# Three of six units of a depthwise convolution on VectorE, LN2's normalisation and a bias on ScalarE, and a product in two 64-row tiles

## The chip, the cores and the metric

One core of one Trainium2 chip runs the whole program. The metric is the device time in microseconds of one execution. Five engines work side by side, each in its own fixed order of instructions: TensorE (PE, with its weight loads PEld), VectorE (DVE), ScalarE (ACT), GpSimd (POOL) and SyncE (SP, which here only issues DMAs).

## The reference

The input is 32 images of 56 x 56 pixels with 96 channels. Every image goes through two layers:

```python
# layer 0: an inverted residual with mixed experts (E = 4, M = 384)
rw = sigmoid(mean(x) @ Wr + br)                  # four weights per image
h = relu(bn1(x @ (rw . Wpw) + rw @ bpw))         # 96 -> 384 channels
h = relu(bn2(sum_e rw[e] * (dw3x3(h, Wdw[e]) + bdw[e])))   # depthwise, 3 x 3, 'SAME'
x = bn3(h @ (rw . Wpwl) + rw @ bpwl) + x         # 384 -> 96
# layer 1: a mixer by Fourier transform over all 3136 tokens, then a feed-forward
t = tokens(x)
u = relu(bn(ln(t) @ w1))                         # 96 -> 192
X = fft(u, axis=tokens, norm='ortho')
xr = relu(X.real * rd - X.imag * id + rb)        # diagonals of r and i
xi = relu(X.imag * rd + X.real * id + ib)
t = t + bn2(ifft(xr + 1j * xi).real @ w2)        # 192 -> 96
z = float8_e5m2(ln(t))                           # LN2 is this ln
z = relu(fp16(fp16(z @ W1) + fp8(b1)))           # 96 -> 384, h in fp16
t = t + fp16(fp16(fp8(z) @ W2) + fp8(b2))        # 384 -> 96
```

## The kernel before

**Staging.** Channels lie on partitions, an image is cut into two halves by columns (h = 0, 1), each with its own padded tile `x0`, `x1`, and each half into two stretches (`st` = 0 to 3). `record(b)` writes down the steps of one image; all 32 are written down before anything is issued.

**The conditional convolution.** The 384 channels are three groups of 128 (c = 0, 1, 2); a half image and a group together are a *unit*, six per image. There are two forms of a unit. `by_tensor` expands 96 to 128 channels in 32-column tiles (`x,wk` 32x435, 16 matmuls), spreads the four pixels of every 2 x 2 square over partitions by DMA (`hp<-h`), convolves as 64 matmuls of 32x32 tiles (`hp,wg`) with weights that GpSimd builds, evicts with bias and relu on ScalarE (`hp<-ps,small`) and sends the result back by DMA (`h<-hp`). `by_vector` expands with full 128-column matmuls (464 and 406 columns), makes the middle tap with its bias on ScalarE (`h<-h,small`), adds eight taps for each of two stretches on VectorE (`h<-h,small,h`, 16 instructions of 784 elements) and ends with a relu on ScalarE (`h<-h`). `BY_VECTOR` says which units are of the second form: group 2 of each half (`DC = 2`). The projection of a half (`project`) runs over the three groups into four banks of PSUM, from 32-row tiles (`h,wk`) or, for a by_vector unit, whole (`h,wkc`); `landed` adds it to `x`.

**The Fourier mixer.** `moments` turns tokens with the identity, takes their statistics on VectorE, and their root on GpSimd (`root`, a power of -1/2). `hidden`, `scaled` and `along_h` make the first transform's direction, which goes through DRAM (`gd`). Then seven groups of frequencies (`GROUPS`: six of four and one of five) each run `along_q` (the second direction: 128 channels in `za`, the last 64 in `zb`, two frequencies sharing one tile of 128 partitions, 64 rows each), nine steps of the filter on ScalarE and VectorE, `second` (the product with `w2`, in one bank for a group of four), `back_q` and a DMA to `yd`.

**The tail.** For each stretch: `back_h`, the residual, `moments` again (LN2), `normal` (seven instructions per stretch, `nt<-ps,ln`), `turn_back`, the feed-forward: `up`, a copy of h to fp16 on ScalarE (`h16`), bias and relu on VectorE (`h<-h,fb`), a cast to fp8 on GpSimd, `down`, bias and residual.

**What sets the order.** Each step is an entry of a `Plan`, with an engine, a cost in microseconds, a due time and the buffers that it takes. `Plan.order()` plays all steps through once before the kernel is built: an engine that comes free takes, of the first 60 ready steps by due time, the first whose buffers are free. The order found is then issued to the engines as it is (`Pinned`), so that the profile puts nearly all instructions on one line, that of the helper. The due times come from `WANT` (a period per image and offsets of the parts), a table of corrections `NUDGE`, one per step in turn, and

```python
if eng in ("DVE", "ACT") and any(isinstance(k[0], Buf) and isinstance(k[0].ring, Banks) for k in reads):
    due -= HURRY
```

which moves the steps that read PSUM ahead. `LAG` is the planner's time from an end to a dependent start on another engine. PSUM is a ring of eight banks (`Banks`), from which a step takes one, two (a neighbouring pair) or four; `r_h` holds three expanded units.

Of the kernel before, what the change touches and what calls it, by code (L numbers as in the profile page):

```python
# [11 lines left out]
F32 = mybir.dt.float32  # L12
F16 = mybir.dt.float16
E5M2 = mybir.dt.float8e5
AF = mybir.ActivationFunctionType
# [3 lines left out]
NE = 4  # L19
C = 96  # L20
# [21 lines left out]
DC = 2  # L42
NT = NC3 - 1
NG = 4 * NT
# [110 lines left out]

LANES = 8
# [4 lines left out]
def packets(n, size):  # L161
# [7 lines left out]
WANT = dict(period=120.2, expand=0.0, vector=1.4, forward=10.7, forward_step=27.0, freq=172.2,  # L169
            freq_step=7.0, tail=259.2, tail_step=26.5, x=17.0, mix=33.5, project=33.0)  # L170

HURRY = 115.8
# [6 lines left out]
    18.3, -16.9, 17.3, 0, -35.5, 15.1, -2.2, -43.4, 13.8, 5.4, 60.8, 7.8, -0.2, -11.5, 4, 4.7, -13.1, -0.5,  # L179
    18.6, 17.1, 11.1, 10.2, -11, 20.5, -10.1, 14.1, -21.4, 3.4, -7.5, 17.2, 4.5, 21.7, 18.3, 11.9, -19.7, 22.1,  # L180
    11.4, 0, -2.1, 49.4, -19.6, 9.4, -26.2, -6.4, 9.1, 3.3, 5.5, 5, 21.1, 20.3, 33.2, -7, 5.8, -11.9,
    16.3, -7.5, 3.9, -11.5, 12.5, -4.7, 8.9, -4.9, 17.9, 27.4, -6.8, 18.5, -3.3, 11.3, 28.7, 17.7, 19.5, 44.7,
    16.4, 1.2, 9.3, -0.3, 19.5, -5.2, 17.7, -40.7, 8.8, -11.7, -4.1, -9.1, -20.5, -7.9, 1.7, 4.5, -4.4, -8.8,
    3.4, 24.1, 10.9, 14.8, 2, -5.6, 1.7, 0.7, -28.5, -26.6, -32.6, -10.9, 13.4, -39.7, 11.4, 3.2, 6.1, -5.6,
    -2.4, -8.8, 4, 16, -5.7, 18.6, 16.8, 28.3, 33, 30.6, 44.6, 31.5, 16.1, 24.8, 20.3, 36.5, 24.6, 16.1,
    18.6, 42.7, 23.9, 27.6, -3.5, 18.6, -17.7, 2.5, 5.3, 14.5, -0.8, -3.7, 17.7, 9.8, -4.6, 2, 0, 23.1,
    3.5, 21.5, 38.9, 28.4, 44.9, 18.8, 22.4, 26.6, -19, -32.5, -1.9, -10.7, -7.8, 9.5, -10.4, -3.8, -2.9, 8,
    18.9, 13.5, 3.1, 7.3, 8.9, 7, 8.1, 16.4, 11.1, -3.4, -3.1, 20.3, -22.7, -7.6, -24.5, -27.4, -36.4, -34.1,
    -7.3, -20.6, 1.7, 21.7, 20.8, 7.7, 9.3, -5.2, 21.2, 1.1, 2, -16.9, -20.2, -3, 25.2, 3, -24.4, -16.8,
    -12.7, -3.5, 8.7, 1, 23.4, 0.5, 36.6, 13.9, -3.3, 18.2, -6, -15.4, -28, -3.3, -1, 17.1, -0.1, -10.8,  # L190
    -6.3, -25.1, 5.2, -1.4, 8.7, 26.7, -2.7, 31.5, -8.7, -20.5, 17.7, 4.2, -5.4, -11.3, -32.3, 6.6, 36.1, -6.7,
    -16, -33, -18.4, -5.3, 5.5, 6, 28.7, 0, 19.4, 2.9, -31.5, 1.2, -19.7, -10.4, -31.4, -34.5, -8.8, 28.8,
    -34.6, -24.7, -20.9, -38.6, -59.8, -23.4, -15.1, -3, -7.9, -34.5, -56.8, -18.7, 2, -3.6, 10.8, -11.1, 7, 8,
    12.5, -7.2, -61.1, -21.9, 10.6, -3.6, 5.1, -0.2, 3.8, -23.7, -10.7, 25.8, -39.1, -3.1, 3.5, 8.3, -0.9, -28.2,
    -40.3, -3.1, 6.2, 5.8, -18.2, 2.1, -4.7, 20.6, 13.6, -4.8, -49.9, -11.8, 33.8, 6.2, 3.1, -12.4, -19.8, -2.2,
    -15.5, 31.7, -33.1, 12, -1.1, 5.2, -15.6, -56.7, -33.2, -4.2, -6, 0.3, -24.5, -5.5, 1.3, 6.7, -3.6, -23,
    -40.1, 0.5, 32.2, 12.1, -12.4, 0.6, -15.2, 1.8, -11.6, 25.9, -25.3, -0.3, -13.6, 11.9, -9.8, -30.8, -60.1, -29.8,
    9.3, 6.2, -6.3, -5.5, -22.1, 12.9, -5.4, -21.4, -61.3, -2.3, 28.4, 10.6, -0.7, -0.3, 2.2, -3.7, -13.8, 45.6,
    -30.6, -1.8, 4.8, 20.9, -13.9, -4.2, -50.9, -12.3, 5.2, 21, -0.3, 0.1, 0.6, 16.1, -14, -20.6, -90.4, -5.2,
    3.7, 4.1, 4.4, -11.5, -3.2, -9.8, -23.9, 38, -24.6, 0.3, -15.5, 7.6, 5, -33.5, -53.7, 2.4, 3.3, 3.5,  # L200
    7.4, 6.3, 12.4, 55.3, 31.8, -20.5, -60.3, -4.5, 17.2, 12.9, 4.9, 11.6, 7.1, -5.1, 6.7, 49.7, -19.7, -2.1,
    12.4, 19.1, -9.6, -27.1, -37, -5.2, 8.4, 12.9, 1, 2.8, -16.1, 18.1, 26.9, 0.5, -23.1, 12.4, -39.5, -5,
    8.3, 3.6, 2.3, -7.3, -10.6, 32.4, 10.2, 3.2, 23.3, -1.6, 4.1, -6.5, 0, 12.6, 37.9, -9.8, -31.5, 2.8,
    5.4, 3.4, -11.1, 10.2, 4.5, 5, -3.7, 14.2, 0.9, -11.5, -3.6, 7.3, 10.4, -10.2, -6.8, 38.5, -53.4, 21.2,
    3, -4, -2.4, 17.2, -7.6, -23.2, -13.5, -17.6, -5.3, 19.8, -18.8, -48.7, 11.7, 1.6, -11, -29.3, 21.3, -5.8,
    -12.2, -1, 41.3, 3.3, -11.9, 3.1, 14.2, 2.1, 3.7, -0.2, 4.7, -56, 58.2, 18.7, 18.6, 18.1, 20.1, -8.6,
    -31.7, -8.6, 13.1, 0.1, 23.5, -8.6, -37.4, 10.2, 2.8, -13.7, -14.1, -4.3, -14.4, 3.5, 2.7, 28.4, 7.8, 5.6,
    -4, -11.5, 1.5, -5.5, 4.2, 2, -45, 20.5, 28.6, 35.4, 4.9, 21.3, -1.2, -21.7, -3.5, -6.1, 0.7, 40.2,
    -17.3, -21.9, 8.1, 1.8, -10.1, 17.2, -4.1, -5.9, -4.4, 3.6, 20.7, 6.6, 5, 16.3, 25.7, 1.8, -8.5, -1.2,
    -26.7, -59.5, 30.7, -19.7,  # L210
# [4 lines left out]
class Plan:  # L215
# [49 lines left out]
    def order(self):  # L265
# [64 lines left out]
        while events:  # L330
            now = events[0][0]
            while events and events[0][0] <= now:
# [3 lines left out]
                elif kind == "end":  # L336
                    for a in x.after:
                        a.left -= 1
                        lag = LAG["SP"] if x.size else 0.0 if a.eng == x.eng else LAG[x.eng]
                        a.ready = max(a.ready, now + lag + a.slack)  # L340
                        if a.left == 0:
                            push(a.ready, "ready", a)
# [39 lines left out]
def kernel(  # L382
# [58 lines left out]
    stk16 = const([128, NE + 1, NSM + 10], F32, "stk16")  # L441
# [4 lines left out]
    w2b = const([128, 2, C], F32, "w2b")  # L446
# [38 lines left out]
    with tc.tile_pool(name="prep", bufs=1) as pp:  # L485
# [65 lines left out]
        nc.vector.memset(w2b, 0.0)  # L551
        nc.scalar.dma_start(w2a[0:C], w2t[:, 0, :])
        nc.scalar.dma_start(w2a[C:128], w2t[0:32, 1, :])
        for j in range(2):
            nc.scalar.dma_start(w2b[64 * j : 64 * j + 64, j], w2t[32:C, 1, :])
# [60 lines left out]
        for c in range(NT):  # L616
# [3 lines left out]
        nc.vector.tensor_scalar_mul(  # L620
            stk16[:, 0:NE, NSM : NSM + 9], rawp[:, 9 * DC : 9 * DC + 9].rearrange("p k e -> p e k"), s2[:, DC : DC + 1]
        )
        nc.vector.tensor_scalar_mul(stk16[:, 0:NE, NSM + 9], rawp[:, 10 * NC3 + DC], s2[:, DC : DC + 1])
        nc.vector.tensor_copy(stk16[:, NE, NSM + 9 : NSM + 10], sh2[:, DC : DC + 1])
# [55 lines left out]
        for j in range(2):  # L680
            nc.vector.tensor_mul(w2b[:, j], w2b[:, j], scrow)
# [29 lines left out]
    r_small = places(2, [128, NSM + 10], F32, "small")  # L711
# [44 lines left out]

    PERIOD = WANT["period"]
    BY_VECTOR = ((0, DC), (1, DC))

# [4 lines left out]
    def record(b):  # L764
# [68 lines left out]
        def mix_wk2():  # L833
# [8 lines left out]
            "DVE", 2.49, t0 - WANT["mix"], lambda: mixed(wk.ap, wpw_s, wpw_s[:, NE], C + 1), port=True,  # L842
# [23 lines left out]
        def by_vector(h, c, due, acc):  # L866

            hv = Buf(r_h)
            edges = (0, 8, 16, 23, 30)
            for i in range(4):  # L870
                ps, n = Buf(banks), edges[i + 1] - edges[i]

                def expand(i=i, n=n, ps=ps):
# [10 lines left out]
                    "ACT", cols("ACT", n * (S + 2)) + 0.12, due - 4,  # L884
# [6 lines left out]
            def taps(i, tap):  # L891
# [3 lines left out]
                return src, to, small.ap[:, NSM + tap : NSM + tap + 1]  # L895

            def first(i):
                src, to, w = taps(i, 4)
                se.activation(to, src, AF.Identity, scale=w, bias=small.ap[:, NSM + 9 : NSM + 10])
# [25 lines left out]
        def by_tensor(h, c, due, hid):  # L925
# [11 lines left out]
            for g in range(4):  # L937
# [3 lines left out]
                def expand(g=g, ps=ps, chan=chan):  # L941
# [14 lines left out]
                    "ACT", cols("ACT", 435), due - WANT["expand"] + 1,  # L956
# [16 lines left out]
            def conv():  # L973
# [13 lines left out]
                "PE", 3.75, due, conv, reads=[(wg, 0), *((hp, r) for r in range(4))],  # L987
# [23 lines left out]
        for h in range(2):  # L1011
# [3 lines left out]
            for c in range(NC3):  # L1015
                if plain[c]:
                    by_vector(h, c, t0 + h * PERIOD / 2 + WANT["vector"], hid[c])
# [561 lines left out]
```

## Time and profile before

| | |
|---|---|
| median of 3 runs | 4438.66 us (4423.89 to 4443.58) |
| the profiled execution | 4444.37 us, span 4442.5 us |
| busy | TensorE 90%, VectorE 80%, ScalarE 56%, GpSimd 32% of the span |
| mean granted TensorE clock | 0.962 |
| DMA | 734.08 MB, 165 GB/s |
| share of the chain that ended last | TensorE 52%, VectorE 18%, ScalarE 10%, DMA 9% |

A row of a group of instructions reads: engine, operation, the tiles written and read (buffer numbers left out; `ps` is PSUM), the shapes, the count, then the busy time in all and the mean duration in ns, then the idle time of the engine just before them and what ended it. A float32 matmul stands in the trace as two rows. Busy time is the union of overlapping instructions, so that sixteen small matmuls side by side count once. A row of waits reads: who waited, for whom, us in total, times, the longest. A row of the timeline: start and length in us, engine, operation, tiles, shape of the first of the piece, how many instructions.

### The profile page before, as it was taken

The page shows a single profiled execution, that of the slowest core. Times are in us where ns is not written, and L with a number is a line of the kernel's source. Part 1 is how long each engine was busy: PE and PEld are TensorE (multiplying, and loading weights), DVE is VectorE, ACT ScalarE, POOL GpSimd, SP SyncE. Part 2 cuts the span into 40 slices and gives each one's busy share as a digit, 9 for nine tenths or more (in the row PEclk, how much of TensorE's full clock was granted, in tenths as well). Part 3 has the DMA queues.
Part 4 walks back from the last instruction along what each step waited for, and adds up shares of the span by engine and source line. Part 5 has one row for each costly group of instructions (what it writes and reads, how often), then busy time and mean ns, then how long its engine had stood idle before and what let it go on. Part 6 is the DMA issues. An engine that isn't in the chain of part 4 may idle for free.

```text
span 4442.5 us, 114026 instructions
## 1 busy us (share of the span) xinstructions
PE 4003.5 (90%) x44802; PEld 2605.1 (59%) x44802; DVE 3535.3 (80%) x9669; ACT 2507.0 (56%) x4975; POOL 1432.2 (32%) x1364
## 2 busy tenths in 40 slices
PE   2998999999999999999999999899999999999985
PEld 1555665566665566666556666566666566565564
DVE  5777887888878888888888787787887887877864
ACT  2455665565665556666556565455665556565543
POOL 1123333333333333333333323333333333233323
PEclk9999999999999999999999998899999999999996
DMA  5876678767778777777877767667778777677752
GB/s 119 178 163 147 159 179 183 164 165 170 165 175 188 172 173 178 166 169 182 184 166 168 171 160 170 151 165 171 164 175 190 167 169 170 153 171 177 162 142 69
DMA packets 440074, 734.08 MB, mean 165 GB/s; under 512 B 159158, under 2 KB 294774, under 8 KB 439494
## 3 DMA queue, kind: packets, MB, share of 16 engines
q1 hardware_dynamic: 433920, 722.30, 70.4%
q8 instruction: 354, 5.80, 0.6%
q10 hardware_dynamic: 5618, 4.49, 0.4%
q14 instruction: 182, 1.49, 0.1%
HBM read 300.21 MB, written 211.04 MB: 115 GB/s over the span
## 4 chain that ended last, share of the span: by engine, by line
PE 52%; DVE 18%; ACT 10%; DMA 9%; issue 4%; POOL 4%; SPq 1%; POOLq 0%; ACTq 0%; DVEq 0%
PE ps L376 52%; DMA g<-gd 6%; POOL ln L376 4%; DVE za L376 3%; ACT h L376 3%; DVE h L376 3%; DVE ha L376 3%; DVE ln L376 2%; DVE tmpa L376 2%; ACT tmpa L376 2%; DVE zb L376 2%; SPq L376 1%; DMA yt<-yd 1%; ACT za L376 1%; DVE tmpb L376 1%
## 5 line engine op out<-in xcount | busy, mean ns | idle before, releaser
L376 DVE SCALAR_TENSOR_TENSOR h<-h,small,h 128x784 f32<-128x784 f32 x1024 | 1064.2, 1051 | 48.5 <-ACT h L376 29.3
L376 POOL CAST h<-h 128x784 fp8e5<-128x784 f16 x384 | 413.9, 1082 | 989.7 <-DVE h L376 986.5
L376 PE MATMUL ps<-x,wk 97*32 97x435 f32 (+2 forms) x4608 | 680.9, 575 | 14.7 <-ACT h L376 11.1
L376 PE MATMUL ps<-hp,wg 32*32 32x392 f32 x16384 | 518.9, 516 | 36.8 <-issue 25.4
L376 PE MATMUL ps<-dftb_s,g 112*128 112x112 f32 (+1 forms) x3776 | 427.2, 284 | 60.8 <-DMA g<-gd 36.1
L376 ACT ACTIVATE h<-ps 128x435 f32<-128x435 f32 (+2 forms) x768 | 397.7, 541 | 109.9 <-PE ps L376 103.1
L376 PEld LDWEIGHTS ps<-dftb_s,g 112*128 112x128 f32 (+1 forms) x3776 | 356.3, 171 | 167.6 <-issue 100.7
L376 POOL TENSOR_TENSOR ln<-ln,mhalf 120x7 f32<-120x7 f32 (+1 forms) x256 | 447.6, 1748 | 21.3
L376 PEld LDWEIGHTS ps<-x,wk 97*32 97x32 f32 (+1 forms) x4608 | 199.5, 119 | 398.1 <-issue 290.1
L376 DVE SCALAR_TENSOR_TENSOR ha<-ps,ln,nshift 120x192 f32<-120x192 f32 x896 | 312.0, 407 | 129.3 <-PE ps L376 124.6
L376 PEld LDWEIGHTS ps<-hp,wg 32*32 32x32 f32 x16384 | 284.6, 105 | 219.7 <-issue 112.8
L376 DVE TENSOR_SCALAR nt<-ps,ln 112x96 fp8e5<-112x96 f32 x896 | 267.2, 368 | 169.3 <-POOL ln L376 169.1
L376 ACT ACTIVATE hp<-ps,small 128x392 f32<-128x392 f32 x512 | 265.5, 589 | 222.1 <-PE ps L376 209.2
L376 ACT ACTIVATE h<-h 128x784 f32<-128x784 f32 x128 | 109.7, 857 | 468.0 <-DVE h L376 467.9
L376 ACT CAST h<-ps 128x784 f16<-128x784 f32 x384 | 306.0, 816 | 105.6 <-PE ps L376 103.9
L376 PE MATMUL ps<-h,wk 32*96 32x392 f32 x4096 | 359.8, 492 | 0.0
L376 PE MATMUL ps<-w1c,x 96*120 96x192 f32 x1792 | 349.4, 336 | 4.8 <-issue 2.7
L376 DVE BATCH_NORM_STATS2 ln<-ps 120x6 f32<-120x96 f32 (+1 forms) x1792 | 315.2, 247 | 44.4 <-PE ps L376 40.2
L376 POOL COPY park<-x 96x784 f32<-96x784 f32 x128 | 109.0, 852 | 747.2 <-DVE x L376 695.3
L376 DVE TENSOR_SCALAR h<-h,fb 128x784 f16<-128x784 f16 x384 | 240.8, 633 | 99.7 <-ACT h L376 99.4
L376 PEld LDWEIGHTS ps<-w1c,x 96*120 96x120 f32 x1792 | 291.1, 186 | 46.0 <-issue 26.5
L376 ACT COPY g<-ps 128x768 f32<-128x768 f32 x256 | 206.1, 807 | 183.1 <-PE ps L376 176.5
(173 smaller groups left out, 7160.8 us busy)
## 6 DMA issues: line engine op xcount, KB each, us to landing
hp<-h SPq DMA_DIRECT2D x512, 217.5 KB
h<-hp SPq DMA_DIRECT2D x512, 196.0 KB
gd<-g SPq DMA_DIRECT2D x384, 192.0 KB
g<-gd SPq DMA_DIRECT2D x192, 336.0 KB
dd<-ddd SPq DMA_DIRECT2D x128, 392.0 KB
yt<-yd SPq DMA_DIRECT2D x128, 336.0 KB
xd<-park SPq DMA_DIRECT2D x128, 294.0 KB
xs<-xd SPq DMA_DIRECT2D x128, 294.0 KB
```

What stands on the lines that cost most here:

```text
L376: return self.tc.keep_in_program_order(method(*args, **kwargs))
```

## The change

1. `BY_VECTOR` becomes three units of six: (0, 2), (1, 1) and (1, 2). The due times of the three are spread at thirds of an image. `VC` lists the groups whose taps `stk16` and `small` hold a second time, two in place of one.
2. LN2's normalisation goes from VectorE (subtract, multiply) to ScalarE (scale and bias). VectorE makes the bias, minus mean times rstd, in one small new step (`shift`).
3. The bias and relu of h (`fb1`) go from VectorE to ScalarE.
4. `w2b` holds the last 64 rows of `w2` once in each half of the partitions, without zeros; `second` multiplies each frequency from its 64 rows, the two halves into two different banks, and takes two banks for every group. A second, small copy evicts the fifth frequency.
5. The costs of some steps, `WANT`, `HURRY` (115.8 becomes 666), the planner's `OWN` (a lag between steps of one engine, new) and all of `NUDGE` are others, so the order of all engines is another.

```diff
-DC = 2
+BY_VECTOR = ((0, 2), (1, 1), (1, 2))
+VC = (2, 1)
...
+OWN = {"DVE": 0.11, "ACT": 0.12}
...
-WANT = dict(period=120.2, expand=0.0, vector=1.4, forward=10.7, forward_step=27.0, freq=172.2,
+WANT = dict(period=113.9, half=60.1, expand=0.0, vector=1.4, forward=10.7, forward_step=27.0, freq=172.2,
...
-HURRY = 115.8
+HURRY = 666.0
...
-                        lag = LAG["SP"] if x.size else 0.0 if a.eng == x.eng else LAG[x.eng]
+                        lag = LAG["SP"] if x.size else OWN.get(x.eng, 0.0) if a.eng == x.eng else LAG[x.eng]
...
-    w2b = const([128, 2, C], F32, "w2b")
+    w2b = const([128, C], F32, "w2b")
...
-        nc.vector.memset(w2b, 0.0)
...
-            nc.scalar.dma_start(w2b[64 * j : 64 * j + 64, j], w2t[32:C, 1, :])
+            nc.scalar.dma_start(w2b[64 * j : 64 * j + 64], w2t[32:C, 1, :])
...
             for c in range(NC3):
                 if plain[c]:
-                    by_vector(h, c, t0 + h * PERIOD / 2 + WANT["vector"], hid[c])
+                    at = BY_VECTOR.index((h, c)) / len(BY_VECTOR)
+                    by_vector(h, c, t0 + 2 * at * HALF + WANT["vector"], hid[c])
             for i, c in enumerate(ours):
-                by_tensor(h, c, t0 + (h + i / len(ours)) * PERIOD / 2, hid[c])
+                by_tensor(h, c, t0 + (h + i / len(ours)) * HALF, hid[c])
...
-            ps, zo = Buf(banks, wide), Buf(r_zo)
+            ps, zo = Buf(banks, 2), Buf(r_zo)

             def second(nk=nk, nb=nb, ps=ps, za=zs[0], zb=zs[1]):
-                for j in range(nb):
-                    ks = range(2 * j, min(2 * j + 2, nk))
-                    to = ps.ap_cols(256 * j, 128 * len(ks))[:PB].rearrange("p (n w) -> p n w", w=128)[:, :, 0:C]
-                    te.matmul(to, zb.ap[:, j, :], w2b[:, 2 - len(ks) :, :], start=True, stop=False)
-                    for e, kk in enumerate(ks):
-                        te.matmul(to[:, e], za.ap[:, kk, :], w2a, start=False, stop=(kk == ks[-1]))
+
+                def to(k):
+                    return ps.ap_cols(512 * (k % 2) + 128 * (k // 2), C)[:PB]
+
+                for k in range(nk):
+                    at = slice(64 * (k % 2), 64 * (k % 2) + 64)
+                    te.matmul(to(k), zb.ap[at, k // 2, :], w2b[at], start=(k < 2), stop=False)
+                for k in range(nk):
+                    te.matmul(to(k), za.ap[:, k, :], w2a, start=False, stop=(k >= nk - 2))
...
+            def seconds(nk=nk, ps=ps, zo=zo):
+                v = ps.pair[:PB].rearrange("p (e j w) -> p j e w", e=2, w=128)[:, :, :, 0:C]
+                se.copy(zo.ap[:, 0:4, :].rearrange("p (j e) w -> p j e w", e=2), v[:, 0:2])
+                if nk > 4:
+                    se.copy(zo.ap[:, 4, :], v[:, 2, 0])
...
+            def shift(ln=ln):
+                mean, rstd = ln.ap[:PB, :, 8], ln.ap[:PB, :, 9]
+                ve.scalar_tensor_tensor(mean, mean, -1.0, rstd, ALU.mult, ALU.mult)
+
             def normal(ps=ps, ln=ln, nt=nt):
                 for q in range(SQ):
-                    ve.tensor_scalar(
-                        nt.ap[:, q, :], ps.piece(q, 128)[:PB, 0:C], ln.ap[:PB, q, 8:9],
-                        ln.ap[:PB, q, 9:10], ALU.subtract, ALU.mult, saturate=False,
+                    se.activation(
+                        nt.ap[:, q, :], ps.piece(q, 128)[:PB, 0:C], AF.Identity, scale=ln.ap[:PB, q, 9:10],
+                        bias=ln.ap[:PB, q, 8:9], saturate=False,
                     )

-            add("DVE", 2.0, due + 4, normal, reads=[(ps, 0), (ln, 0)], writes=[(nt, 0)], takes=[nt])
+            add("DVE", 0.1, due + 3, shift, writes=[(ln, 0)])
+            add("ACT", 2.1, due + 4, normal, reads=[(ps, 0), (ln, 0)], writes=[(nt, 0)], takes=[nt])
...
                 add(
-                    "DVE", 0.333, due + 9,
-                    lambda c=c, h16=h16: ve.tensor_scalar(
-                        h16.ap, h16.ap, fb1[:, c : c + 1], 0.0, ALU.add, ALU.max
-                    ),
-                    port=True, writes=[(h16, 0)],
+                    "ACT", 0.86, due + 9,
+                    lambda c=c, h16=h16: se.activation(h16.ap, h16.ap, AF.Relu, bias=fb1[:, c : c + 1]),
+                    writes=[(h16, 0)],
                 )
```

## The prediction

> **What bounds the kernel now.** I read the page's totals first, then the busy time by stretches, then the groups of instructions with shapes kept apart, then the waits, the chain of waits, and the timeline of TensorE for the steps that the change touches.
>
> ```profile
> span 4442.5 us, 114026 instructions
> PE 4003.5 (90%) x44802; PEld 2605.1 (59%) x44802; DVE 3535.3 (80%) x9669; ACT 2507.0 (56%) x4975; POOL 1432.2 (32%) x1364
> ```
>
> ```profile
> 2000.00:2500.00 500.00, 462.91 (x5371) 304.82 (x5370) 410.78 (x1126) 296.29 (x590) 166.71 (x160) 0.98 0.76 175
> ```
>
> The columns are TensorE, its weight loads, VectorE, ScalarE and GpSimd busy, the granted clock, the DMA share and GB/s. The seven stretches from 500 to 4000 us are alike: 3250 of 3500 us busy on TensorE (93%), 2866 on VectorE (82%), 2060 on ScalarE (59%). The chain of waits shows one TensorE piece of 20.7 us (279 instructions) in every image, from 1203.07 to 2646.11 us eleven images later: 131.2 us per image. So an image is 121.8 us of TensorE work and 9.4 us in which it idles; VectorE works 107.4 us, ScalarE 77.2. 32 images are 4198 us, the filling and draining the other 244. TensorE is the bound, VectorE close behind, ScalarE has room. The profiled execution took 4444.37 us, 1.9 over its span and 0.13% over the median of the runs (4438.66); I add to it.
>
> ```profile
> PE ps L376 <- ACT h L376: 96.7, 120, 1.3
> PE ps L376 <- DVE ha L376: 39.2, 32, 1.3
> PE ps L376 <- DMA g<-gd: 36.1, 28, 3.2
> DVE nt L376 <- POOL ln L376: 169.1, 122, 3.1
> ```
>
> TensorE's rows of this view, summed by releaser: some 130 us end with a ScalarE step (4.1 per image), 109 with VectorE (46.5 of it in the prologue, so 2.0 per image), the rest with GpSimd, DMA and issue.
>
> **The third unit on VectorE.** A unit is a third of the channels of one half image. By the counts in the engines' orders each image loses one unit of 64 matmuls 32x392, one unit of expansion in 32-column tiles and one of projection from 32-row tiles, and gains the plain forms:
>
> ```profile
> L376 PE MATMUL ps<-hp,wg 32*32 32x392 f32 x16384 | 518.9, 516 | 36.8 <-issue 25.4 <-DMA hp<-h 5.3 <-POOL wg L376 0.6
> L376 PE MATMUL ps<-x,wk 97*32 97x435 f32 x4096 | 456.2, 576 | 0.0
> L376 PE MATMUL ps<-h,wk 32*96 32x392 f32 x4096 | 359.8, 492 | 0.0
> L376 PE MATMUL ps<-h,wkc 128*96 128x392 f32 x512 | 194.8, 522 | 0.0
> L376 DVE SCALAR_TENSOR_TENSOR h<-h,small,h 128x784 f32<-128x784 f32 x1024 | 1064.2, 1051 | 48.5 <-ACT h L376 29.3
> ```
>
> The first three rows serve 128 units: 4.05 + 3.56 + 2.81 = 10.42 us each. The plain unit costs 194.8/64 = 3.04 for its projection and (123.9 + 122.1)/64 = 3.84 for its expansion (the two forms of 464 and 406 columns): 6.88. TensorE gains **3.54 us** per image, on the engine that sets the end. VectorE gets 16 more passes of 1.051 us: +16.8. ScalarE gets 2 x 1.064 (first tap) + 2 x 0.857 (relu) + 2 x (0.566 + 0.517) = 6.0 in place of 4 x 0.542 + 4 x 0.589 = 4.5: +1.5. Eight DMAs and their issues on the SP queue go (54 of 734 MB in all), and one GpSimd weight build of 1.08: both lay beside other work, 0 for the time. VectorE's three units are due at thirds of the image, and in its new order the passes are scattered between the other steps instead of standing ten in a row ahead of the projection; so I count no new wait for them.
>
> **LN2 and the bias to ScalarE.**
>
> ```profile
> L376 DVE TENSOR_SCALAR nt<-ps,ln 112x96 fp8e5<-112x96 f32 x896 | 267.2, 368 | 169.3 <-POOL ln L376 169.1
> L376 DVE TENSOR_SCALAR h<-h,fb 128x784 f16<-128x784 f16 x384 | 240.8, 633 | 99.7 <-ACT h L376 99.4
> L376 ACT ACTIVATE h<-h 128x784 f32<-128x784 f32 x128 | 109.7, 857 | 468.0 <-DVE h L376 467.9
> L376 ACT ACTIVATE zb<-ps,fb 128x112 f32<-128x112 f32 x192 | 87.5, 456 | 14.0 <-DVE tmpb L376 10.4 <-DVE zb L376 3.6
> ```
>
> VectorE loses 267.2/32 = 8.35 and 240.8/32 = 7.5 per image and gets four small shifts at the 0.17 of its other ln steps, 0.7: with the 16.8 it ends 1.6 higher, at 109.0. ScalarE's normalise (PSUM source, scale and bias from columns) is nearest to the last row, 0.456 for 112 elements; four like it in a row took 2.02 us where one takes 0.589, so about 0.11 of each overlaps: 0.33 each for 96 elements, 28 per image, 9.3. The ends are 28 x 0.22 = 6.2 (the plain PSUM copy's 0.475 for 384 and 0.559 for 480 elements, run down to 96) and 28 x 0.44 = 12.4. The bias with relu is nearest to the relu of the same size, 12 x 0.857 = 10.3. ScalarE: 77.2 + 1.5 + 9.3 + 10.3 = 98.3 us per image.
>
> The row says that VectorE's biased step costs 0.63 and ScalarE's 0.86, so the pair is dearer after the move; but ScalarE has the room and VectorE hasn't. The Trainium skill, "ScalarE: Activation LUTs" (Rules for kernel authors), speaks against the move outright: relu and add belong on VectorE, up to three times faster on 16-bit data. By the rows the 12 steps cost 12 x 0.23 = 2.8 us more of engine time, by that rule (a third of 0.86) 6.9, and in neither case any of TensorE's. The rows don't show its three times: VectorE's 0.63 is a mean with waits beside GpSimd, 0.40 the least.
>
> The wait that moves: normalise waits for GpSimd's root, 169.1 us on VectorE now (5.3 per image). VectorE's shift now takes it, then ScalarE waits for the shift. Queued behind the normalise on ScalarE are evictions of PSUM, for which TensorE waits. At 0 if the order puts filler between, at 5.3 if all of it stands: I take 0, since 98.3 us leave ScalarE room in an image, and keep 5.3 for the rivals.
>
> **The last 64 channels in two 64-row tiles.** In the timeline of TensorE:
>
> ```profile
> 2107.74 0.55 PE L376 MATMUL ps<-w2b,zb 128*112 128x192 f32 x2 [0.27 <-DVE zb L376]
> 2108.13 0.54 PE L376 MATMUL ps<-w2a,za 128*112 128x96 f32 x4
> 2108.51 0.51 PE L376 MATMUL ps<-w2b,zb 128*112 128x192 f32 x2
> 2108.85 0.54 PE L376 MATMUL ps<-w2a,za 128*112 128x96 f32 x4
> 2109.22 1.49 PE L376 MATMUL ps<-w1c,x 96*120 96x192 f32 x8
> ```
>
> ```profile
> 2197.90 0.99 PE L376 MATMUL ps<-dftb_s,g 112*64 112x112 f32 x16
> 2198.82 0.79 PE L376 MATMUL ps<-ident,x 96*120 96x96 f32 x7
> ```
>
> From start to start, a group of four frequencies takes 1.48 us now: 2 x 0.36 for the padded product w2b and 2 x 0.38 for w2a (0.095 per row; a matmul has two rows in the trace). Afterwards w2b is four half-height matmuls, 8 rows of 96 columns. The trace has no 64-row tiles of this width; nearest are the 64-column tiles above: 16 rows in 0.92, elsewhere 8 rows in 0.54, so 0.0475 a row of 112 columns and 0.16 fixed. That makes 8 x 0.041 + 0.16 = 0.49, with w2a's 0.76 it is 1.25: 0.23 less. The group of five goes from 1.80 to 0.57 + 0.95 = 1.52. Six and one per image: **1.66 us**. If the tiles don't run together, 0.76 + 0.76 = 1.52, a loss of 0.3 per image; without the fixed part, a gain of 2.6.
>
> The fixed 0.16 stands in the row. The Trainium skill, "TensorEngine Tiling (Array Packing)" (Key Properties), has a reason for such a term, that a change of tiling mode drains the engine, and under Gotcha 1 warns that row tiles need different PSUM banks; it prices neither.
>
> Each group of four now takes a pair of banks where it took one: 6 more banks for some 2.5 us each, 15 bank-us of the 8 x 131 that an image has, while the lost unit gives back four banks for about 6 us, 24. So 0.
>
> **The order.** Every eviction now comes ahead of anything else that is ready on its engine (its due time goes back by 666 instead of 116), and each step has another due time. What that does to the 9.4 us of idle no row shows: below zero is possible, since 4.1 of it waits for ScalarE; above zero too, since VectorE goes from 82% to 87% of a shorter image and ScalarE from 59% to 78%. I take zero between them.
>
> **The sum.** 3.54 + 1.66 = 5.2 us of TensorE per image, 166 in 32; 4444.4 - 166 = **4278 us**. The other engines stay below the new 126 us (VectorE 109, ScalarE 98).
>
> **Rivals.**
> 1. *Waits grow with the load.* ScalarE's hand-offs cost TensorE 4.1 us at 59%, VectorE's 2.0 at 82%. If both together grow by half, 3.0 per image come back: 4374 us (band 4326 to 4416). For it: three engines near 80% or more. Against: ScalarE's load alone does not make the waits, the less busy engine has the more of them.
> 2. *ScalarE blocks TensorE, slower.* The normalise stands in ScalarE's queue until GpSimd's root is done: the whole 5.3 us reach TensorE through the evictions behind it, and the 4.1 double. +9.4 - 5.2 = +4.2 per image, 4578 us. It is slower from 5.9 us of added idle on. Against: the longest such wait is 3.1 us, and evictions can be ordered ahead of it.
> 3. *The order finds more.* Evictions first, and the DMA round trip of one unit gone: the 4.1 halve, 2.05 per image, 4212 us (band 4130 to 4230). For it: the largest releaser on TensorE is the eviction of h.
> 4. *It cancels.* Idle grows by just what the work shrinks by, 4.5 to 5.9 per image: 4444 us.
>
> **How the numbers follow.** 0.5% of this kernel, 22 us, is about what a measurement can tell. The forecast (4230 to 4326, idle within 1.5 us of 9.4) has 0.54, rival 1 0.17, rival 2 0.11, rival 3 0.12, rival 4 0.06. The unknown tiles (4247 to 4340) lie within the first two. Faster: 0.54 + 0.17 + 0.12 = 0.83; same 0.06; slower 0.11. From 4190 to 4405 lie the forecast, rival 1 but for a little, and most of rival 3: about 0.8.
>
> **What would show it.** Right: TensorE about 3840 us busy, still over 92% in the middle stretches; VectorE about 3585; ScalarE about 3180; nt on ScalarE near 0.44 us each, w2b with w2a near 1.25 a group. Wrong: ScalarE releasing more than 6 us of TensorE's idle per image, long rows of ScalarE waiting for ln, w2b's rows at 0.095 each, or an image over 130 us.

## The result, and the profile after

The changed kernel took 4391.28 us (median of six runs, 4381.36 to 4411.1) where the kernel before, beside it, took 4441.45: a ratio of 0.9894, 95% interval 0.9866 to 0.9922. It is faster by about 50 us; the forecast was 166. The sign was right, the size a third. The profiled execution took 4390.8 us. In all that follows, an execution more than 1.5% above the fastest of its kernel, at a lower granted clock, is left out of its median.

The first two rows of the changed kernel's page, and its row in the view by stretches (columns as in the prediction):

```profile
span 4389.0 us, 104599 instructions
...
PE 3988.9 (91%) x40066; PEld 2522.6 (57%) x40066; DVE 3551.2 (81%) x9036; ACT 3110.9 (71%) x6281; POOL 1632.2 (37%) x1332
```

```profile
2000.00:2500.00 500.00, 466.83 (x4776) 294.98 (x4773) 411.35 (x1031) 361.92 (x734) 191.99 (x154) 0.96 0.70 162
```

TensorE lost 4736 of its 44802 matmul rows, but only 14.6 us of busy time, where 166 were forecast. The rest of the gain came from idle time, for which the forecast had nothing: 439.0 us before (span less busy time), 400.1 after. VectorE and ScalarE came out close to the forecast (3551 for 3585, 3111 for 3180). So the engines that were given work behaved; the engine that was relieved hardly got less busy. The groups, again from the page:

```profile
L380 DVE SCALAR_TENSOR_TENSOR h<-h,small,h 128x784 f32<-128x784 f32 x1536 | 1557.0, 1050 | 103.3 <-ACT h L380 84.5
...
L380 ACT ACTIVATE h<-h,fb 128x784 f16<-128x784 f16 x384 | 361.1, 965 | 1.3
...
L380 ACT ACTIVATE nt<-ps,ln 112x96 fp8e5<-112x96 f32 x896 | 301.7, 436 | 62.6 <-DVE ln L380 58.7
```

A pass on VectorE still takes 1.05 us, a normalising step on ScalarE 0.436 (0.44 forecast); the bias step takes 0.965, an eighth more than the 0.857 it was priced at. GpSimd, whose share was put at nothing, is busy 1632 us in place of 1432, though it builds fewer weights: its casts of h average 1.34 us, 1.08 before. And the waits, the first three TensorE's, the last VectorE's:

```profile
PE ps L380 <- ACT h L380: 61.6, 121, 2.1
PE ps L380 <- issue: 49.0, 24, 4.1
...
PE ps L380 <- POOL h L380: 31.7, 15, 10.6
```

```profile
DVE ln L380 <- POOL ln L380: 125.9, 96, 3.0
```

Summed by releaser, TensorE waited 109 us for ScalarE (130 before), 67 for VectorE apart from the prologue (109 before), 32 for GpSimd (19) and 79 for DMAs (74). The new load on ScalarE did not turn into waits. "issue" grew from 34.2 us to 49.0: time in which TensorE stood still and nothing that the profile shows held it.

The loss is not spread evenly. Taking the first `ones,nsa` matmul of each image's frequency stage as a mark, the first mark came at 226.6 us in place of 213.3, the images 0 to 3 took 550.0 us in place of 525.1, and from image 4 on an image took 129.8 us on average (133.3 before), but in a cycle: 126 to 128 us for about five images, then up to 140, again and again every ten images.

### The profile page after: what moved, and what is told of

Same layout as the page of the kernel before. It is cut to its first block, busy times and chain, and to the rows that moved or that the text cites. A ratio compares the mean times of both kernels' runs of the same rounds, so it can differ in the third digit from the quotient of the medians.

```text
span 4389.0 us, 104599 instructions
## 1 busy us (share of the span) xinstructions
PE 3988.9 (91%) x40066; PEld 2522.6 (57%) x40066; DVE 3551.2 (81%) x9036; ACT 3110.9 (71%) x6281; POOL 1632.2 (37%) x1332
## 4 chain that ended last, share of the span: by engine, by line
PE 46%; ACT 19%; DVE 13%; DMA 9%; POOL 6%; issue 4%; SPq 1%; POOLq 0%; ACTq 0%; DVEq 0%
PE ps L380 46%; ACT h L380 6%; ACT nt L380 5%; POOL ln L380 5%; DVE ln L380 3%; DVE ha L380 3%; ACT tmpa L380 2%; DMA hp<-h 2%; DMA yt<-yd 2%; DMA da<-dad 2%; DVE za L380 2%; DVE tmpa L380 2%; DVE h L380 1%; ACT tmpb L380 1%; ACT y L380 1%
## 5 line engine op out<-in xcount | busy, mean ns | idle before, releaser
L380 DVE SCALAR_TENSOR_TENSOR h<-h,small,h 128x784 f32<-128x784 f32 x1536 | 1557.0, 1050 | 103.3 <-ACT h L380 84.5
L380 POOL CAST h<-h 128x784 fp8e5<-128x784 f16 x384 | 511.2, 1335 | 738.3 <-ACT h L380 738.3
L380 PE MATMUL ps<-hp,wg 32*32 32x392 f32 x12288 | 420.4, 520 | 48.6 <-DMA hp<-h 28.1
L380 POOL TENSOR_SCALAR ln<-ln 120x7 f32<-120x7 f32 (+1 forms) x256 | 130.0, 508 | 866.4 <-DVE ln L380 866.4
L380 ACT ACTIVATE h<-h,fb 128x784 f16<-128x784 f16 x384 | 361.1, 965 | 1.3
L380 PEld LDWEIGHTS ps<-hp,wg 32*32 32x32 f32 x12288 | 218.7, 105 | 232.0 <-issue 106.9
L380 ACT ACTIVATE nt<-ps,ln 112x96 fp8e5<-112x96 f32 x896 | 301.7, 436 | 62.6 <-DVE ln L380 58.7
L380 PEld LDWEIGHTS <-fw 96*128 96x128 fp8e5 (+1 forms) x1536 | 155.5, 115 | 315.7 <-issue 214.6
L380 ACT ACTIVATE hp<-ps,small 128x392 f32<-128x392 f32 x384 | 202.1, 598 | 178.2 <-PE ps L380 163.0
L380 POOL TENSOR_TENSOR xs<-xs,y 96x784 f32<-96x784 f32 x128 | 238.1, 1860 | 238.6 <-DVE y L380 238.6
```

Of the source, the lines that this page charges most:

```text
L380: return self.tc.keep_in_program_order(method(*args, **kwargs))
```

## The experiments

Three theories came out of the traces. **Tiles:** the two 64-row tiles save almost nothing. **Ends:** the first images lose what later images gain. **Fetches:** TensorE stops for its own instructions, which makes the cycle. The rivals: the tiles save what the sum says; the gain per image is simply smaller everywhere; ScalarE's load has eaten it.

### The tiles undone

```diff
-                    te.matmul(to(k), zb.ap[at, k // 2, :], w2b[at], start=(k < 2), stop=False)
+                    te.matmul(both, zb.ap[:, j, :], w2b[:, 2 - len(ks) :, :], start=(j != 1), stop=False)
...
```

> The changed kernel, its w2b product again as one padded matmul per pair of rows (w2b in two copies, one half of each zero), in the same pair of banks; every other operation and the order as in the changed kernel. The traces say: the two 64-row tiles save about 0.05 us in a group of four (1.43 against 1.48) and cost 0.1 in the group of five (1.91 against 1.80), 0.2 to 0.3 an image, so this kernel should be 4391 plus 0 to 15 us. By the sum in the prediction (1.66 us an image saved by the tiles) it should be 53 us slower than the changed kernel, 4444.

Measured: 4396.24 us (0.9905 of before, 0.9881 to 0.9929), 5 us over the changed kernel, where the sum's term wanted 53. TensorE's timeline for one group of four, changed kernel first, then the padded one:

```profile
1436.21 0.64 PE L380 MATMUL ps<-w2b,zb 64*112 64x96 f32 x8
1436.78 1.03 PE L380 MATMUL ps<-w2a,za 128*112 128x96 f32 x8
1437.64 0.50 PE L380 MATMUL ps<-h,fw 128*96 128x392 fp8e5 x2
```

```profile
1421.14 0.83 PE L380 MATMUL ps<-w2b,zb 128*112 128x192 f32 x4
1421.80 0.93 PE L380 MATMUL ps<-w2a,za 128*112 128x96 f32 x8
1422.57 0.50 PE L380 MATMUL ps<-h,fw 128*96 128x392 fp8e5 x2
```

From start to start the tiles take 0.57 and the padded form 0.66; the following w2a takes 0.86 behind the tiles and 0.77 behind the padded product. What the tiles win, the next product loses. Over all groups of four at full clock the medians are 1.51 us before, 1.51 here, 1.43 in the changed kernel (1.25 forecast); for the single group of five 1.98, 2.00 and 1.91 (the prediction had 1.80 for it before, 1.52 after). Once an image two groups stand back to back: 3.27 us before, 2.92 here, 2.95 changed, so there the tiles lose. Over all rows of w2b and w2a at full clock (the count is explained below) it is 356.7 us before, 350.4 here and 341.9 in the changed kernel: 15 us of the 53, 6 of which come with the order of the rows, all w2b ahead of all w2a, that the padded kernel keeps. The weight loads are a likely reason why half the height gains so little; no run tests them alone (groups by shape: busy us in all, mean ns of one; the changed kernel, then two rows of the kernel before):

```profile
L380 PEld LDWEIGHTS ps<-w2b,zb 64*112 64x112 f32 x1856 | 114.9, 177 | 73.0 <-DVE ln L380 22.0 <-DVE za L380 16.3 <-DVE zb L380 7.5
```

```profile
L376 PEld LDWEIGHTS ps<-w2b,zb 128*112 128x112 f32 x960 | 139.0, 182 | 133.4 <-ACT h L376 71.5 <-DVE zb L376 30.0 <-issue 9.9
L376 PEld LDWEIGHTS ps<-dftb_s,g 112*64 112x64 f32 x1920 | 103.4, 140 | 58.1 <-issue 46.0 <-DVE zb L376 0.6 <-DVE tmpb L376 0.6
```

A load of 64 rows and 112 columns takes 177 ns, one of 128 rows 182, and the tiles need twice as many. They overlap in pairs, so all of them together come to 114.9 us for 139.0. The last row is the product that the forecast took its price from: its loads are half as *wide*, and take 140 ns.

### Twelve images

Edit: `NB = x.shape[0]` becomes `NB = 12`, in both kernels.

> The kernel before, only the first 12 of the 32 images (the other outputs stay unwritten). Worked out from its trace: frequency stage of image 11 at 1664, less 25 because the last image runs faster, plus 132 of draining and 2: 1774 us (1755 to 1790).

> The changed kernel, only the first 12 of the 32 images (the other outputs stay unwritten). If the missing gain is lost while the pipeline fills and drains, as the traces say, 1677 - 28 + 139 + 2 = 1790 us, that is 16 us SLOWER than 12 images of the kernel before (5 to 30). If instead each image gains the same 1.1% wherever it stands, as a smaller gain per image would have it, 12 images are 20 us faster than 12 of the kernel before, about 1754.

Measured: 1783.17 us before, 1808.31 changed. The changed kernel is 25 us *slower* over twelve images. The other twenty took 4436.88 - 1783.17 = 2653.7 us before (132.7 each) and 4391.28 - 1808.31 = 2583.0 changed (129.1 each). So the gain is 3.5 to 3.6 us an image once the pipeline runs, and the first twelve, which should have brought 42 us at that rate, lose 25: by this count 67 us are missing there. Part of it belongs to the short program: behind the last mark it runs 153.8 us (132.5 in the kernel before), while the changed kernel with all images needs 139.4 (132.6 before). The loss of 25 was sharper than expected (16) and rules out an even smaller gain everywhere.

### LN2 and the bias back on VectorE

```diff
...
-            add("ACT", 2.1, due + 4, normal, reads=[(ps, 0), (ln, 0)], writes=[(nt, 0)], takes=[nt])
+            add("DVE", 2.0, due + 4, normal, reads=[(ps, 0), (ln, 0)], writes=[(nt, 0)], takes=[nt])
...
-                    "ACT", 0.86, due + 9,
-                    lambda c=c, h16=h16: se.activation(h16.ap, h16.ap, AF.Relu, bias=fb1[:, c : c + 1]),
+                    "DVE", 0.333, due + 9,
+                    lambda c=c, h16=h16: ve.tensor_scalar(
+                        h16.ap, h16.ap, fb1[:, c : c + 1], 0.0, ALU.add, ALU.max
+                    ),
...
```

> The changed kernel with the LN2 normalise and the bias of h back on VectorE (7 normalising instructions a strip of 0.27 us and 3 bias additions of 0.33 us, no shift instruction), the third unit still on VectorE, the order planned anew with the same offsets. VectorE gets about 12 us an image more, 121 of 128. If the move to ScalarE is what makes room for the third unit, the image grows by 3 to 12 us: 4490 to 4780. If ScalarE's load had eaten the gain (a rival), taking it back makes the kernel faster than 4391.

Measured: 4761.71 us, 370 over the changed kernel (1.0739 of before, 1.0704 to 1.0774). The order was not searched again for it, so its size is an upper bound for the move; its sign is clear. VectorE is then busy 4053 us, as long as TensorE (4088), and TensorE idles 656 us (400 in the changed kernel). The two moves went back together, so what each is worth is not shown.

### The cycle: one alignment per image

The rows of TensorE from mark to mark (matmuls, weight loads and 30 semaphore rows) number 2534 in every steady image of the changed kernel and 2830 before. The page lists a queue of instructions,

```profile
q8 instruction: 316, 5.18, 0.5%
```

316 packets of 16.4 KB, 9.9 per image: one for about 256 rows. With 2534 rows an image starts 26 rows earlier in a block than the image before it, and is back after 9.85 images, the length of the cycle. Sorted by the mark's row number modulo 256, the steady images are:

```
position   76 - 132: 126.1 to 127.8 us     position 210 - 254: 129.2 to 132.0 us
position  150 - 206: 125.9 to 128.0 us     position   2 -  54: 132.4 to 139.6 us
```

The padded kernel above has 2478 rows per image (82 rows earlier each time) and a cycle of three: 126, 138, 131. In the timeline of image 12 of the changed kernel a convolution breaks off after 106 of its 128 rows:

```profile
1890.28 3.81 PE L380 MATMUL ps<-hp,wg 32*32 32x392 f32 x106
1897.36 1.25 PE L380 MATMUL ps<-hp,wg 32*32 32x392 f32 x22 [3.27 <-issue]
```

An instruction packet began 0.8 us into those 3.27 us. It is the rule: of the 20 stops of more than 1 us that the changed kernel has under "issue", 17 have such a packet, which lands 1.1 to 1.8 us before TensorE goes on. And the stop is not the whole price. Just ahead of it the granted clock is full; behind it, it is half for 10 us (columns as above):

```profile
1891.10:1894.00 2.90, 2.90 (x106) 1.51 (x73) 0.42 (x1) 0.09 (x1) 1.68 (x1) 1.00 0.96 130
1897.90:1907.90 10.00, 10.00 (x71) 7.84 (x55) 4.52 (x20) 3.39 (x6) 1.53 (x2) 0.50 0.57 115
```

At that clock 14 rows of `w1c,x` take 4.83 us, elsewhere 2.54:

```profile
1898.54 4.83 PE L380 MATMUL ps<-w1c,x 96*120 96x192 f32 x14
...
1457.53 2.54 PE L380 MATMUL ps<-w1c,x 96*120 96x192 f32 x14
```

Between 420 and 4200 us, 15 of the 18 stops have a stretch at half clock within 3.6 us behind them. To make it an experiment, the position was fixed, at four offsets:

```diff
                 def along_q(blk=blk, n=n, k0=k0, nk=nk, ps=ps, g2=g2):
+                    if k0 == 0 and blk == 0:
+                        te.addr_align(256, offset=0, max_nops=255)     # 0, 64, 128, 192
```

> The changed kernel with one alignment directive at the frequency stage of each image: TensorE's next instruction is put at slot 0 of a block of 256 instructions, with no-operations in the gap, some 26 an image (2534 instructions an image become 2560, ten blocks). Every image then meets the block boundaries at the same places. In the changed kernel images took 126 to 140 us in a cycle of ten. If TensorE's instruction fetches make that cycle, the cycle vanishes: all images of one run agree within 2 us, at one value between 126 and 140, and the four offsets differ, some near 126.5 (about 4300 us in all, 3.3 us times 27 images below 4391) and one or more at 135 to 139 (4540 to 4650). If the cycle has another cause (the order, the clock, the DMAs), it stays and all four are alike, at 4391 plus at most 1 us an image for the no-operations.

> As the run at slot 0, with the aligned instruction at slot 64. The same two expectations; which of the four offsets is fast is not known beforehand, but fast phases were 130 of 256 wide in the changed kernel, so two of the four should be fast.

> As the run at slot 0, with the aligned instruction at slot 128. The same two expectations.

> As the run at slot 0, with the aligned instruction at slot 192. The same two expectations.

| slot | median us | ratio to before (interval) | steady images us |
|---|---|---|---|
| 0 | 4320.53 | 0.9711 (0.9671 to 0.9752) | 125.4 to 128.0, two of 132 |
| 64 | 4559.35 | 1.0263 (1.0225 to 1.0301) | 130.4 to 139.8 |
| 128 | 4395.25 | 0.9888 (0.9851 to 0.9925) | 127.4 to 130.8 |
| 192 | 4325.3 | 0.9735 (0.9703 to 0.9768) | 125.9 to 128.3, one of 132.7 |

The cycle of ten is gone, and the same work in the same order takes 4320 or 4559 us by where the block boundaries fall. (At the bad slot the images differ by more than the 2 us expected.) TensorE's waits at slots 0 and 64:

```profile
PE ps L380 <- issue: 40.9, 7, 15.9
```

```profile
PE ps L380 <- issue: 164.1, 55, 16.2
```

At slot 0, 33 of the 40.9 us are the no-operations of the first two images and the last, where the gap is not 26 but up to 255. So the directive was kept to images 2 to 30:

```diff
+                    if k0 == 0 and blk == 0 and 2 <= b < 31:
+                        te.addr_align(256, offset=0, max_nops=40)      # 0, 224
```

> The changed kernel aligned at slot 0 as in the run at slot 0 (4320.5), but only from image 2 to image 30, and with at most 40 no-operations executed, a longer gap being jumped over. In the run at slot 0 TensorE stood 8.0, 16.0 and 8.8 us in up to 255 no-operations before the frequency stages of images 0, 1 and 31. Without them: 4320.5 - 33 + about 3 for one jump = 4290 us (4280 to 4305), 0.966 of before. If those stalls were covered by other waits of the filling, 4320.

> The same at slot 224, between the two fast offsets (192: 4325, 0: 4320). If the price of a place of the block boundary is smooth, as the images of the changed kernel by their position were, 4280 to 4300 us.

Measured: 4293.2 us (0.9662, 0.9637 to 0.9688) and **4280.02 us (0.9639, 0.9618 to 0.9660)**, as expected. The second beats both kernels. Its images 4 to 29 take 125.4 to 128.9 us; its wait and page rows:

```profile
PE ps L380 <- issue: 3.5, 2, 2.3
```

```profile
span 4278.2 us, 105328 instructions
...
PE 3906.9 (91%) x40066; PEld 2474.4 (58%) x40066; DVE 3554.2 (83%) x9036; ACT 3109.4 (73%) x6281; POOL 1632.2 (38%) x1332
```

The same 40066 rows now count 82 us less busy time than in the changed kernel. Most of this is the clock: TensorE works 229 us in stretches at half clock, 371 in the changed kernel, and half of the 142 us between them, 71, is what the lower clock adds (an estimate).

The same for the kernel before (gaps over 16 slots jumped over):

> The kernel before with the same directive from image 2 to 30 at slot 0, gaps over 16 slots jumped over: its 2830 instructions an image become 3072 slots, 12 blocks, 242 of them jumped over each image. Its images took 128 to 143 us, mean 132.7, in a cycle of 18. Locked, all should agree within 2 to 3 us at one value: 129 to 139, plus up to 3 us for the jump, 4350 to 4700 in all. If only the changed kernel suffers from fetches, this one stays at 4440 plus the jumps and keeps its cycle.

> The kernel before locked at slot 128. One of its two offsets should be on the fast side (about 129 to 131 us an image with the jump, 4340 to 4400); the better of the two, against the better of the changed kernel's, tells what the change is worth at equal luck with the fetches: by the ledger 3 us an image less the 68 us of filling and draining, so 30 to 60 us.

Measured: 4487.34 and 4458.49 us (1.0097, 1.0070 to 1.0124; 1.0041, 1.0009 to 1.0074). Neither offset was a fast one, a miss. At slot 0 the images agree within 4 us (132.8 to 136.9), but each jump stops TensorE for 3.2 us (2.9 to 3.6) before the frequency stage:

```profile
PE ps L376 <- issue: 96.8, 46, 3.6
```

The jumps are 91 us of it, in 28 images, so the rest of such an image took about 131.8. They don't cost all of that: the wait for `g` at the same place, 36.1 us before, is gone. At slot 128 the ten runs lie between 4436 and 4503. What the change is worth at equal luck with the fetches stays open.

### The ends

Edit: `NB = 1`; in the third kernel the unit (1, 1) also goes back to `by_tensor` with its steps 60 us later than due, in the fourth LN2 and the bias go back to VectorE as above.

> The kernel before, image 0 alone (the other outputs stay unwritten): filling and draining and nothing else. From its trace 213 to the frequency stage, 132 after it, 2 around: about 347 us (335 to 355).

> The changed kernel, image 0 alone: from its trace 227 + 139 + 2 = 368 us, 20 us more than the kernel before (10 to 25). If the longer filling came only from images that overlap, both are alike within 3 us.

> As the changed kernel's lone image, with the third unit (channels 128 to 255 of the second half) back on TensorE, the other offsets kept. If VectorE's passes of the third unit hold up the lone image, 10 to 17 us less than the changed kernel's lone image; if it is the ScalarE move or the order, the same within 3 us.

> As the changed kernel's lone image, with LN2's normalise and the bias of h back on VectorE, the third unit staying there. The chain of a strip loses some 0.1 us of shift, 0.2 of normalise and 3 times 0.6 of bias: with the four strips of the draining one after the other 3 to 8 us less than the changed kernel's lone image; nothing if these stand beside other work.

Measured: 319.59 us (317.22 and 321.96), 329.34 (328.23 to 331.32), 329.96 and 324.51 (322.44 to 326.88). A lone image is 10 us longer after the change, not 20, and part of this may be the granted clock, which was 0.81 and 0.80 before and 0.78 after; the third unit has no part in it; with LN2 and the bias back, 5 us of the 10 go, which is near the limit of what the runs tell. The estimates were 27 and 39 us too high because a mark in the full program has work of the next images ahead of it; a later first mark is therefore not by itself a loss. So much of the 67 us must arise where images overlap. To see it at the start, `NB = 3`, and in the second kernel the third unit of image 0 back on TensorE, its steps 80 us later than due:

```diff
-            plain = [(h, c) in BY_VECTOR for c in range(NC3)]
+            units = BY_VECTOR if b >= 1 else ((0, 2), (1, 2))
+            plain = [(h, c) in units for c in range(NC3)]
...
```

> The changed kernel, images 0 to 2 alone (the other outputs stay unwritten): from its trace 227 + 137 + 108 + 139 + 2 = 613 us; the same sum was 37 us too high for a lone image, so 575 to 615.

> As the changed kernel's three images, with the third unit of image 0 alone back on TensorE; images 1 and 2 as they are. If the third unit of image 0 holds up TensorE where the images overlap (TensorE waited 9 us there for weights mixed on VectorE, 5 us for x, where the kernel before waited 3), 6 to 17 us less than the changed kernel's three images; if it is the searched order of the rest, within 3 us.

Measured: 629.29 us (624.64 to 630.35) and 616.65 (609.63 to 618.05): image 0's third unit costs 12.6 us once other images overlap it, with the order planned anew. TensorE's waits in the two, with the unit on VectorE and without it in image 0:

```profile
PE ps L380 <- POOL h L380: 28.5, 13, 11.2
...
PE ps L380 <- DVE wk L380: 9.2, 2, 6.0
```

```profile
PE ps L381 <- POOL h L381: 24.0, 15, 3.5
...
PE ps L381 <- DVE wk L381: 5.4, 2, 3.2
```

TensorE waits 4 us less for the mixed expansion weights of the next image (`wk`, mixed on VectorE), and the one wait of 11.2 us for GpSimd's cast of h is gone.

## Why the prediction was right in sign and wrong in size

**How TensorE's time is counted here.** Over all matmul rows of a trace, each counts from its start to the start of the next row, or to its end where TensorE then stands idle; the sum is the page's busy time. Half of what falls into stretches at half clock is put down to the clock, the rest is work at full clock. The four profiled executions, in us:

| | before | changed | slot 224 | slot 64 |
|---|---|---|---|---|
| work at full clock | 3856 | 3803 | 3792 | 3803 |
| added by the lower clock | 147 | 186 | 115 | 257 |
| idle | 439 | 400 | 371 | 513 |
| span | 4442.5 | 4389.0 | 4278.2 | 4572.8 |

So the work shrank by 53 us where 166 were forecast, the clock took 38 of them back, and idle time, put at zero, gave 39. That the sign came true is half luck: without the idle time 15 us would be left. Where the block boundaries fall changes the second and third rows and leaves the first almost as it is.

**The third unit: the first step that failed, in its size.** The products of the expansion, the convolution and the projection took 1692.5 us of work before and 1642.7 after: 50 us less, where 3.54 an image, 113, were forecast. The unit that went was priced rightly: 10.04 us by this count for a unit in tiles and 6.36 for a plain one, 3.69 apart. But the sum took the price of the units that stay as given, and the 96 units that are still in tiles took 10.91 each: +0.47 in the projection, +0.28 in the convolution, +0.12 in the expansion. The same 64 rows of the projection, both times at full clock, before and after:

```profile
2122.95 5.52 PE L376 MATMUL ps<-h,wk 32*96 32x392 f32 x64
```

```profile
1414.22 6.54 PE L380 MATMUL ps<-h,wk 32*96 32x392 f32 x64
```

In the first the four tiles start within 0.02 us of each other, every time; in the second some rows start alone, up to 0.56 us before the next. It goes with the place in the order: in the changed kernel a convolution of 128 rows takes (median, at full clock) 3.6 us behind the plain projection or behind `h,fw`, and 4.9 behind the plain expansion, where a third of them now stand. Fixing the packets' position does not cure it (10.76 a unit at slot 224). What puts the tiles out of step no run singles out.

VectorE took its 16 passes at the price named. "No new wait" was not quite so: VectorE's passes waited 84.5 us for ScalarE's part of h, 29.3 before, 1.7 us more an image; VectorE's room covered it.

**LN2 and the bias: zero, as far as the waits tell.** ScalarE's releases of TensorE fell from 130 to 109 us, so rivals 1 and 2 did not happen. The wait for the root is still VectorE's, 125.9 us in place of 169.1, and ScalarE now waits 58.7 us for the shift. The bias step was 0.108 us dearer than priced, which ScalarE's room covered. On a lone image the move costs some 5 us.

**The tiles: the second step that failed.** The term of 1.66 us an image, 53 in all, came from the 64-column tiles of another product, whose rows were 0.0475 us. The 64-row tiles ran at 0.071 a row, and the product behind them took 0.09 us longer than it does behind the padded one. Of the 53 us, 15 came, 9 of them from the tiles; the run with the padding back says 5, uncertain by some 15. The neighbour was wrong: it has as many rows, but narrower weights, whose loads are shorter, and the price of the next product was not in the sum at all.

**The rest of the work.** Products that the change does not touch took 12 us more, and the sum had no term for them: `ha,da` 31 more and `zo,dftc_s` 13 more against 30 less for `ident,nt`. By the table, all the terms: 113 became 50, 53 became 15, nothing became -12, and then -38 for the clock and +39 for idle: 54 against the 53.5 between the spans.

**The order, put at zero.** Idle time fell by 39 us, though "issue" grew by 15: TensorE no longer waits for `g<-gd` (36.1 us) and less for ScalarE and VectorE. That is the direction of rival 3, at a smaller size; the order is the likely cause, but no run changes it alone.

**The filling.** "244 us stay" was taken with no working. From mark to mark an image gains 3.5 us (133.3 to 129.8, images 4 to 29); 32 such gains are 113 us, and 59 of them are lost at the ends: 13 before the first mark, 39 in the images 0 to 3 (25 us longer instead of 14 shorter), 7 behind the last mark and the 4 of one image, less 4 that image 30 gains. Images 2 and 3 took 137.8 us each, and 127.3 and 126.5 once the position is fixed from image 2 on: 22 of the 39 are the packets' position. The 10 us of the lone image and the 12.6 of image 0's third unit lie among these 59 and may overlap each other; what is left is not singled out. The two ways of counting, by work, clock and idle and by images, divide the same loss and are not to be added.

**The base.** 131.2 us per image was read from eleven images that lie between two slow stretches of the kernel's own cycle; twenty images measure 132.7. The idle that "no row shows" was partly in the waits under "issue", which the prediction added up with the rest and asked nothing of. Its 109 us for VectorE are the rows without the prologue's 46.5, so VectorE's hand-offs cost TensorE 3.4 us an image, not 2.0, and rival 1 would have come to 4398 instead of 4374.

**The sign that was named and came true:** TensorE's busy time (3989 for 3840) and w2b with w2a at 1.43 a group for 1.25 showed the sum wrong at first sight. That the aligned kernel takes 4280 us, nearly the forecast, is chance: of its 164 us between the spans 64 are work, 33 are the clock and 68 idle time, and the forecast had only work.

## What to carry to other kernels

A price per unit that is read from one order of an engine's work need not hold in another: price a tile form together with the products around it, and check the forms that stay as well as the one that goes. Count an engine's busy time at full clock before comparing it. Keep "filling and draining stay" as a term with a working of its own: a shorter program tells it (a dozen images, one image) for little. In a long unrolled program, sort the time per image by the instruction count modulo the size of a fetched block; where it cycles, a change of a few instructions per image moves the time by more than the change itself is worth, and fixing the position can be a gain without touching the work: it was one at four of the six settings tried in the changed kernel, and at neither of two in the kernel before.

## What the runs showed of the hardware

- TensorE's instructions come in packets of 16.4 KB, about 256 trace rows. By the position of the boundaries alone one and the same kernel took 4320 to 4559 us. Between the changed kernel and the one aligned at slot 224 lie 111 us: 82 of busy time, some 71 of them added by the lower clock (an estimate), and 29 of idle time (45 less under "issue", 17 more in other waits). The granted clock was 0.931 on average at the worst slot, 0.950 in the changed kernel, 0.966 at slot 224. Which stretch makes a boundary dear was not tried apart; the stops stood in the convolution, in `dd,yt` and in `w1c,x`.
- A stop of 2 to 4 us cost more than itself: behind the one of 3.27 us TensorE worked 10 us at half clock, which is 5 us of work lost (an estimate).
- The same run of small tiles has no fixed price: 64 rows of `h,wk` took 5.52 and 6.54 us, 128 rows of `hp,wg` 3.6 and 4.9, at full clock, by their place in the order of TensorE's work.
- A no-operation on TensorE: 16.0 us for at most 255, so at least 0.063 us each (an estimate from the first alignments). Some 26 per image in front of the frequency stage left no gap in the trace there. A jump over 242 slots stopped TensorE for 3.2 us.
- A weight load of 64 rows took as long as one of 128 (177 and 182 ns); one of 64 columns took 140.
